# Relation-weighted graph layers on Trainium2: edge sums that run on over tiles

## The chip, the cores and the metric

One Trainium2 chip, of which one core is used. The metric is the device time of one execution in microseconds (us), the median of the runs shown. Less is better. The kernel is written in Bass and Tile: instructions are issued on five engines, PE (TensorE), DVE (VectorE), ACT (ScalarE), POOL (GpSimd) and SP (SyncE, which only issues transfers), and each engine works through its own instructions in order.

## The reference

Four residual blocks on x, 10000 nodes of 512 floats, one after another. Only the first matters here: two graph layers with relations (RGCN) over 5000 edges of two types.

```python
def rgcn_gate_layer(x, row, col, edge_type, basis, att, gate_w, root, bias):
    w = jnp.einsum('rb,bio->rio', att, basis)          # 2 relations, 30 bases of 512 x 512
    x_j = x[col]
    msgs = []
    for r in range(2):
        gate = jax.nn.sigmoid(x_j @ gate_w[r, :, 0])
        msgs.append(gate[:, None] * x_j @ w[r])
    msg = jnp.where((edge_type == 0)[:, None], msgs[0], msgs[1])
    agg = jax.ops.segment_sum(msg, row, num_segments=x.shape[0])
    return agg + x @ root + bias

h   = relu(rgcn_gate_layer(layernorm(x), ..., basis1, att1, gate_w1, root1, bias1))
x   = x + rgcn_gate_layer(h, ..., basis2, att2, gate_w2, root2, bias2)
x   = x + experts(layernorm(x))       # mixture of 16 experts
x   = x + gine(layernorm(x))          # four graph layers over the same edges by target
x   = x + ternary_ffn(layernorm(x))
```

`row` (the target of a sum) is drawn at random and unsorted, so with 10000 nodes and 5000 edges most targets have one edge, or none.

## The kernel before, in words

**The stages.** The profile's windows follow the program: 0 to 534 us a pass over the nodes, with the sorting of the edges and the relation weights between it; 534 to 842 us the edges of layer 1; 842 to 1096 us the edges of layer 2; after that the second node pass, the experts, four GINE layers and the ternary network, which the diff doesn't touch.

**The node pass.** `rgcn_nodes1` (L725) goes over 20 blocks `b` of 512 nodes. Each loads `x_in`, stores it unchanged to `a2_d` (L733; layer 2's sums are added to these rows later), normalizes it, stores the result to `xn_d`, transposes it, multiplies it by `root` (L742), adds the bias on POOL (L748) and stores to `r1_d`, to which layer 1's sums are added later.

**The relation weights.** `relation_weights` (L625) loads the 30 bases of a layer, 1 MB each, and adds each, times a coefficient, to the weights of both relations on DVE (L635 and L637, 128x2048 elements an instruction, two for a basis).

**Sorting.** `sort_edges` puts the edges in a table by relation and target (`by_src`), and again by target alone for the GINE layers (`by_dst`). The table's 128-row tiles are whole tiles of one relation: the second relation starts on a new tile, so there are `RT = ET + 1 = 41` tiles. `add_targets` makes `sidx`, the row that each edge slot adds to: the first slot of a target within a tile takes the target's row, every other slot a spare row behind the nodes, `N` + partition. `place_nodes` is a generator, taken in small steps between other work; it orders the nodes for the GINE layers.

**The edges.** `rgcn_edges` (L640) runs the same loop for both layers. A tile's way, in the functions' names:

- `fetch(t)`: POOL gathers 128 source rows of 512 floats into `x` (L614).
- `make_ready(t)`: in layer 2 a relu on ACT (L665); two products with the gates on DVE that also sum (`prod`, L669); sigmoid on ACT (L674, `g`); the gate of the edge's own relation on DVE (L675, `dots`); PE transposes the keys (L680, `ps_k`); DVE compares and scales (L682): `same[i, j]` is edge i's gate where edges i and j of the tile have one target, and zero elsewhere.
- `add_up(t)`: PE multiplies `x` by `same` (L689), which sums the edges of a target within the tile and leaves the sums transposed; ACT copies them to `aT` (L693).
- `put(t)`: PE multiplies `aT` by the weights of the tile's relation (L703; a register holds which), ACT copies the product to `o` (L708), POOL adds its rows to DRAM with an indirect DMA (`scatter_add`, L619): to `r1_d` in layer 1, to `a2_d` in layer 2.

A target whose edges lie in two tiles is added to by two scatters. All scatters of a layer write one DRAM tensor, so each waits until the one before it has landed.

The loop's iteration `i` issues `fetch(i)`, `add_up(i - 5)`, `put(i - 6)`, `make_ready(i - 3)`, then perhaps a step of `place_nodes`. For PE, POOL, ACT and DVE the order within this loop is kept as written (`manual_schedule`). SP's order, and everything outside these loops, is the scheduler's: it places the sorting and the weights among the node pass. Some 30 of the 116 adding operations at L637 stood among layer 1's first tiles, the others before.

Of the kernel before, what the change touches and what calls it, by code (L numbers as in the profile page):

```python
# [17 lines left out]
P = 128  # L18
N = 10000
D = 512  # L20
# [5 lines left out]
EDGE_SLOTS = ET * P  # L26
LO = 256
HI = (N + LO - 1) // LO
RT = ET + 1

PAIRS = [(p * 1024, 512) for p in range(N // 1024)] + [(N // 1024 * 1024, N % 1024 // 2)]
PT = 8
# [10 lines left out]
CAP = 625  # L43
CT = (CAP + P - 1) // P
LAYERS = 4
FETCHED, READY = 6, 3
LN_EPS = 1e-5
BN_EPS = 1e-5
# [21 lines left out]
def gnn_ffn_kernel(ctx: ExitStack, tc: tile.TileContext, I, out, dram):  # L70
# [7 lines left out]


    xn_d = dram("xn_d", [N, D])  # L80
    r1_d = dram("r1_d", [N + P, D])
    a2_d = dram("a2_d", [N + P, D])
    xf_d = dram("xf_d", [N + P, D])
    x2_d = dram("x2_d", [N + P, D])
    xg_d = dram("xg_d", [N, D])
# [41 lines left out]
    nc.vector.memset(eps_t, LN_EPS)  # L127

    def clear_spare(zero, d):
        nc.sync.dma_start(d[N:, :], zero)  # L130


    def rows_to(sb, d, b, store=False):
# [83 lines left out]
    def sort_edges(tag, key_d, partner_d, attr_d, table, wk, ps, keep, by_relation=False):  # L217
# [77 lines left out]
        if by_relation:  # L295

            first_r = wk.tile([P, P], F32, name="first_r")
            nc.vector.tensor_scalar(off[:, 1:2], ip, float(HI), None, op0=OP.is_lt)
            nc.vector.tensor_scalar(first_r, ones, off[:, 1:2], None, op0=OP.mult)
            ps_o = ps.tile([P, LO], F32, name="ps_s")  # L300
            nc.tensor.matmul(ps_o[:hr, :1], lhsT=first_r[:hr, :hr], rhs=total[:hr], start=True, stop=True)
            n_i = wk.tile([P, 3], I32, name="n_i")
            nc.vector.tensor_scalar(n_i[:hr, 0:1], ps_o[:hr, :1], float(P - 1), None, op0=OP.add)
            nc.vector.tensor_scalar(n_i[:hr, 1:2], n_i[:hr, 0:1], 7, None, op0=OP.logical_shift_right)
            nc.vector.tensor_scalar(n_i[:hr, 2:3], n_i[:hr, 1:2], 7, None, op0=OP.logical_shift_left)
            nc.vector.tensor_copy(off[:hr, 1:2], n_i[:hr, 2:3])
# [62 lines left out]
        nc.vector.tensor_copy(gidx, srt[:, :, 1])  # L369
        return dict(meta, key=key, gidx=gidx, attr=srt[:, :, 2])  # L370

    def add_targets(meta, wk, ps, keep):

        key = meta["key"]
        first = wk.tile([P, RT], F32, name="before")
        equal_keys(key, RT, below, first, wk, ps)
        w = wk.tile([P, RT], F32, name="w_se")
        nc.vector.tensor_scalar(first, first, 0.0, None, op0=OP.is_equal)
        nc.vector.tensor_scalar(w, key, float(N), None, op0=OP.is_lt)
        nc.vector.tensor_mul(first, first, w)  # L380
        spare = wk.tile([P, RT], F32, name="spare")
        nc.vector.tensor_scalar(spare, ip.to_broadcast([P, RT]), float(N), None, op0=OP.add)
        nc.vector.tensor_sub(w, key, spare)
        nc.vector.tensor_mul(w, w, first)
        nc.vector.tensor_add(w, w, spare)
        sidx = keep.tile([P, RT], I32, name="sidx")
        nc.vector.tensor_copy(sidx, w)
        return dict(meta, sidx=sidx)

    def place_nodes(meta, wk, ps, keep):  # L390

# [6 lines left out]

        key = meta["key"]
        tno = irow[:, :ET]  # L400

        ends = wk.tile([P, 2, ET], F32, name="ends")
        for i, sel in enumerate((first_sel, last_sel)):
            ps_l = ps.tile([P, LO], F32, name="ps_s")
            nc.tensor.matmul(ps_l[:, :ET], lhsT=sel, rhs=key, start=True, stop=True)
            nc.vector.tensor_copy(ends[:, i], ps_l[:, :ET])
        carried = keep.tile([P, 4, ET], F32, name="carried")
        co, stays, passes, enters = (carried[:, i] for i in range(4))
        nc.vector.memset(carried, 0.0)
        nc.vector.tensor_tensor(co[:, : ET - 1], ends[:, 1, : ET - 1], ends[:, 0, 1:], OP.is_equal)  # L410
        nc.vector.tensor_scalar(stays, co, -1.0, 1.0, op0=OP.mult, op1=OP.add)

        nc.vector.tensor_tensor(passes, ends[:, 0], ends[:, 1], OP.is_equal)
        nc.vector.tensor_mul(passes, passes, co)
        nc.vector.tensor_mul(passes[:, 1:], passes[:, 1:], co[:, : ET - 1])
        nc.vector.tensor_sub(enters[:, 1:], co[:, : ET - 1], passes[:, 1:])
        yield

        ahead = wk.tile([P, ET], F32, name="ahead")
# [203 lines left out]


    def relation_weights(basis, att_d, pool, stream, tag):  # L625
        att = row_broadcast(pool, att_d, RELATIONS * BASES, f"att_{tag}")
        ws = pool.tile([P, RELATIONS, KC * D], F32, name=f"w_{tag}")
        for b in range(BASES):
            t = stream.tile([P, KC, D], F32, name="basis")
            nc.sync.dma_start(t, basis[b].rearrange("(k p) o -> p k o", p=P))  # L630
            tf = t.rearrange("p k o -> p (k o)")
            for r in range(RELATIONS):
                c = att[:, r * BASES + b : r * BASES + b + 1]
                if b == 0:
                    nc.vector.tensor_scalar(ws[:, r], tf, c, None, op0=OP.mult)  # L635
                else:
                    nc.vector.scalar_tensor_tensor(ws[:, r], tf, c, ws[:, r], op0=OP.mult, op1=OP.add)  # L637
        return ws

    def rgcn_edges(tag, meta, src_d, relu, ws, gate_d, dst_d, beside, take):  # L640

        with ExitStack() as s:
# [11 lines left out]
            got, ready, sums = {}, {}, {}  # L656

            def fetch(t):
                got[t] = wk.tile([P, D], F32, name="x", bufs=FETCHED + 2)
                gather(got[t], src_d, meta["gidx"][:, t : t + 1])  # L660

            def make_ready(t):
                x, kt = got[t], meta["key"][:, t : t + 1]
# [21 lines left out]
            def add_up(t):  # L685
# [6 lines left out]
                sums[t] = wk.tile([P, KC, P], F32, name="aT")  # L692
                nc.scalar.copy(sums[t], ps_a)  # L693

            def put(t):
                aT = sums.pop(t)
                w0 = nc.values_load(
# [8 lines left out]
                    )  # L706
                o = wk.tile([P, D], F32, name="o")
                nc.scalar.copy(o, ps_o)  # L708
                scatter_add(dst_d, meta["sidx"][:, t : t + 1], o)

            E_ = mybir.EngineType
            with tc.manual_schedule(engines={E_.PE, E_.Pool, E_.Activation, E_.DVE}):
                for i in range(RT + FETCHED):
                    if i < RT:
                        fetch(i)
                    if i >= FETCHED - 1 and i - FETCHED + 1 < RT:
                        add_up(i - FETCHED + 1)
                    if i >= FETCHED:
                        put(i - FETCHED)
                    if READY <= i < RT + READY:  # L720
# [31 lines left out]

    with ExitStack() as s:
        wpool = s.enter_context(tc.tile_pool(name="w_rel", bufs=1))
        stream = s.enter_context(tc.tile_pool(name="stream", bufs=2))
        src_meta = s.enter_context(tc.tile_pool(name="src_meta", bufs=1))
        wk = s.enter_context(tc.tile_pool(name="sort", bufs=1))
        place_wk = s.enter_context(tc.tile_pool(name="place_wk", bufs=1))
# [1 line left out]
        with ExitStack() as n:  # L760
# [18 lines left out]
                meta_pool,  # L779
            )  # L780
            rgcn_nodes1(root, bias, (ld, tp, small, pt, po))
            ws = relation_weights(I["L0_gnn_basis1"], I["L0_gnn_att1"], wpool, stream, "1")
        placing = place_nodes(by_dst, place_wk, ps, meta_pool)
        rgcn_edges(
            "1", by_src, xn_d, False, ws, I["L0_gnn_gate_w1"], r1_d, placing,
            lambda i: i >= FETCHED and i % 2 == 0,
        )
        ws = relation_weights(I["L0_gnn_basis2"], I["L0_gnn_att2"], wpool, stream, "2")
        rgcn_edges("2", by_src, r1_d, True, ws, I["L0_gnn_gate_w2"], a2_d, placing, lambda i: True)
        for _ in placing:  # L790
            pass

# [1081 lines left out]
```

## Time and profile before

| what | value |
|---|---|
| median of 3 runs | 4619.68 us (4619.44 to 4631.54) |
| profiled execution | 4620.11 us, span 4618.3 us |
| mean granted TensorE clock | 0.937 of full speed |
| busy: PE, PEld, DVE | 4021.0, 2037.0, 2799.6 us (87%, 44%, 61%) |
| busy: ACT, POOL | 1723.0, 1548.1 us (37%, 34%) |
| weights L637 (DVE) | 116 operations, 316.3 us |
| `put` L703 (PE) | 656 matmuls of both layers, 304.1 us |

The profiled execution is one execution seen by the hardware profiler; its span goes from the first to the last recorded instruction. Matmuls overlap each other and their ends are modelled, so that PE's busy share overstates how full it is. In the rows, `x12` is a count, `128x512<-128x512` are partitions by elements out and in, and what stands in brackets at a row's end is the idle time of the engine before it and what ended that: another engine's instruction, a DMA, or "issue", for which the profile shows no wait. DVE is VectorE, PEld the loading of weights into PE. The granted clock is the share of full speed that TensorE was allowed.

### The profile page before, as it was taken

What the parts mean: (1) busy time and instruction counts of PE and PEld (TensorE: products, weight loads), DVE (VectorE), ACT (ScalarE), POOL (GpSimd) and SP (SyncE); (2) the same over time, 40 slices, a digit from 0 to 9 for tenths busy, and PEclk for the clock granted to TensorE, in tenths of its full rate; (3) what the DMA queues carried; (4) which work ended last, traced back from release to release, by engine and by line L of the source; (5) the groups of instructions that cost most, each with busy time, mean ns of one, the idle gap of its engine ahead of it and who ended that gap; (6) DMA issues with size and microseconds to landing.
All of it is one profiled execution on the core that took longest, in us unless ns stands there. A gap on an engine that the chain in (4) does not pass through costs nothing.

```text
span 4618.3 us, 42924 instructions
## 1 busy us (share of the span) xinstructions
PE 4021.0 (87%) x13624; PEld 2037.0 (44%) x13624; DVE 2799.6 (61%) x5886; ACT 1723.0 (37%) x3086; POOL 1548.1 (34%) x1124
## 2 busy tenths in 40 slices
PE   6799568897999953996879999999999999999997
PEld 3443234443444421443444545545455455544443
DVE  7888865553545455655765546654576455755776
ACT  4334112232333311114544523344233532335775
POOL 3434334342000034785563113311142111422443
PEclk9899789898989875998989999999999999999998
DMA  8777755456555422897621123102231012311332
GB/s 281 232 259 248 226 127 89 83 105 169 197 170 182 158 64 59 160 162 208 199 71 51 73 77 116 47 19 80 83 111 38 28 76 107 89 31 48 110 112 97
DMA packets 294560, 558.83 MB, mean 121 GB/s; under 512 B 41376, under 2 KB 72129, under 8 KB 293311
## 3 DMA queue, kind: packets, MB, share of 16 engines
q1 hardware_dynamic: 221072, 367.30, 23.5%
q0 software_dynamic: 73264, 188.79, 17.7%
q8 instruction: 111, 1.82, 0.2%
q14 instruction: 113, 0.93, 0.1%
HBM read 295.03 MB, written 260.95 MB: 120 GB/s over the span
## 4 chain that ended last, share of the span: by engine, by line
PE 37%; DVE 9%; DMA 3%; issue 2%; ACT 2%; POOL 1%; POOLq 0%; DVEq 0%; ACTq 0%; SPq 0%
PE ps_b L1340 15%; PE ps_d L1340 9%; PE ps_o L1646 5%; PE ps_e L1340 4%; PE ps_x L1482 2%; PE ps_x L1268 2%; DVE stats L1455 2%; DMA x<-xg_d,gpos 1%; DVE feat L1272 1%; DMA x_in<-x_d,node_at 1%; PE ps_q L1714 1%; DVE feat L1355 1%; DVE x L1257 1%; DVE t L1386 1%; POOL e L1261 1%
## 5 line engine op out<-in xcount | busy, mean ns | idle before, releaser
L1340 PE MATMUL ps_b<-feat,w 128*128 128x512 f32 (+1 forms) x1120 | 499.1, 588 | 6.9 <-ACT feat L1468 6.9
L1340 PE MATMUL ps_d<-feat,w_s 128*128 128x512 f32 (+1 forms) x1096 | 490.7, 584 | 2.2 <-DVE feat L1387 1.3
L1348 ACT ACTIVATE feat<-ps_b,cols 128x512 f32<-128x512 f32 (+1 forms) x300 | 204.1, 682 | 535.2 <-PE ps_b L1340 522.5
L1394 POOL TENSOR_TENSOR feat<-feat 128x1024 f32<-128x1024 f32 (+1 forms) x70 | 162.7, 2324 | 627.0 <-DVE feat L1393 601.9
L637 DVE SCALAR_TENSOR_TENSOR w<-basis,att,w 128x2048 f32<-128x2048 f32 x116 | 316.3, 2736 | 14.9 <-DMA basis<-in_L_gnn_basis 14.9
L742 PE MATMUL ps_o<-root,xT 128*128 128x512 f32 (+1 forms) x632 | 322.2, 622 | 0.0
L1409 POOL TENSOR_TENSOR feat<-feat,p 128x1024 f32<-128x1024 f32 (+1 forms) x66 | 166.7, 2525 | 449.2 <-ACT feat L1348 449.0
L1340 PEld LDWEIGHTS ps_b<-feat,w 128*128 128x128 f32 x1120 | 209.9, 192 | 240.8 <-issue 209.5
L703 PE MATMUL ps_o<-w,aT 128*128 x656 | 304.1, 608 | 0.0
L1484 DVE TENSOR_TENSOR x_rows<-ps_x,be 128x512 f32<-128x512 f32 (+1 forms) x237 | 157.5, 685 | 232.3 <-PE ps_x L1482 232.0
L918 PE MATMUL ps_n<-root,rT 128*128 128x512 f32 (+1 forms) x632 | 288.9, 613 | 0.0
L1340 PEld LDWEIGHTS ps_d<-feat,w_s 128*128 128x128 f32 x1096 | 198.4, 191 | 194.2 <-issue 173.0
L1340 PE MATMUL ps_b<-t,w_s 128*128 128x512 f32 (+1 forms) x560 | 253.2, 592 | 26.1 <-ACT feat L1348 26.1
L614 POOL DMA_INDIRECT x<-xg_d,gpos x160 | 175.6, 1098 | 260.8 <-PE ps_x L1268 50.8
L1340 PE MATMUL ps_e<-feat,w 128*128 128x512 f32 (+1 forms) x560 | 253.9, 592 | 9.3 <-DVE feat L1303 9.3
L1340 PE MATMUL ps_b<-feat,w_s 128*128 128x512 f32 (+1 forms) x560 | 250.0, 585 | 0.0
L1468 ACT ACTIVATE feat<-feat,bn_sm 128x512 f32<-128x512 f32 (+2 forms) x320 | 238.0, 808 | 3.6 <-DVE bn_sm L1446 3.6
L1455 DVE BATCH_NORM_STATS2 stats<-feat 128x6 f32<-128x512 f32 (+1 forms) x320 | 203.6, 667 | 41.4 <-POOL feat L1409 28.3
L1268 PEld LDWEIGHTS ps_x<-same,x 128*128 128x128 f32 x1280 | 165.5, 197 | 110.7 <-ACT x L1263 48.8
L1268 PE MATMUL ps_x<-same,x 128*128 128x128 f32 x1280 | 172.9, 284 | 46.8 <-ACT x L1263 33.1
L170 DVE BATCH_NORM_STATS2 ln_st<-x_in 128x6 f32<-128x512 f32 (+1 forms) x237 | 159.6, 683 | 63.0 <-DMA x_in<-x_d,node_at 59.0
L1263 ACT ACTIVATE x<-x 128x512 f32<-128x512 f32 x160 | 98.9, 628 | 242.4 <-DVE x L1257 174.2
(492 smaller groups left out, 7649.4 us busy)
## 6 DMA issues: line engine op xcount, KB each, us to landing
basis<-in_L_gnn_basis SPq DMA_DIRECT2D x60, 1024.0 KB
xg_d<-x_rows SPq DMA_DIRECT2D x234, 256.0 KB
xg_d<-x_in SPq DMA_DIRECT2D x39, 512.0 KB
x_in<-in_x SPq DMA_DIRECT2D x19, 1024.0 KB
a_d<-x_in SPq DMA_DIRECT2D x19, 1024.0 KB
xn_d<-xn SPq DMA_DIRECT2D x19, 1024.0 KB
r_d<-o_nodes SPq DMA_DIRECT2D x19, 1024.0 KB
r_in<-r_d SPq DMA_DIRECT2D x19, 1024.0 KB
```

The lines of the kernel that those rows point to most:

```text
L614: return nc.gpsimd.indirect_dma_start(out=dst, out_offset=None, in_=src, in_offset=bass.IndirectOffsetOnAxis(ap=idx, axis=0))
L637: nc.vector.scalar_tensor_tensor(ws[:, r], tf, c, ws[:, r], op0=OP.mult, op1=OP.add)
L703: nc.tensor.matmul(ps_o, lhsT=aT[:, k, :], rhs=w_all[:, bass.ds(w0 + k * D, D)], start=k == 0, stop=k == KC - 1,)
L742: nc.tensor.matmul(ps_o[:n], lhsT=xT[:, k, a * P : a * P + n], rhs=root[:, k, :], start=k == 0, stop=k == KC - 1,)
L918: nc.tensor.matmul(ps_o[:n_], lhsT=rT[:, k, a * P : a * P + n_], rhs=root[:, k, :], start=k == 0, stop=k == KC - 1,)
L1268: nc.tensor.matmul(ps_a[:, k, :], lhsT=x[:, k * P : (k + 1) * P], rhs=same, start=True, stop=True)
L1340: nc.tensor.matmul(ps[fo], lhsT=A[a][:, k, fo * P : (fo + 1) * P], rhs=x[:, k, :], start=first and k == 0, stop=k == 1, skip_group_check=True,
L1348: nc.scalar.activation(dst[:, fo, :], ps[fo], func, bias=b, scale=scale)
L1409: (nc.vector if last else nc.gpsimd).tensor_tensor(b22, b22, p5, OP.add)
L1455: nc.vector.bn_stats(stats[:, k, 2 * p + j, :], big[:, k, s0 + j * w : s0 + (j + 1) * w])
L1468: nc.scalar.activation(hb, hb, AF.Relu, bias=sm[:, fo, 3:4], scale=sm[:, fo, 2:3])
L1646: nc.tensor.matmul(ps_o[:n_], lhsT=big[:, kc, t * P : t * P + n_], rhs=W2[kc], start=kc == 0, stop=kc == KC - 1,)
```

## The change

It has four parts.

1. **Sums run on over tiles.** Between the two relations there is now one wholly empty tile (`RT` is 42). `add_targets` finds by the first and last key of each tile whether a target goes on into the next tile (`ends_of` and `carries`, taken out of `place_nodes`). A new step `carry(t)` in `rgcn_edges` adds the running sum of the last tile to the first column of `aT`, or hands it on, with two DVE instructions of 128x4. Slots whose target goes on into the next tile take a spare row, so that each target is added to by one scatter alone. Spare rows are two sets of 128, for odd and even tiles. Each scatter is declared independent of the one before it.
2. **Plain rows copied DRAM to DRAM.** `rgcn_nodes1` no longer stores `x_in` to `a2_d`. In layer 1's loop, 40 transfers of 250 rows (512 KB) on SP's queue copy x to `a2_d`; the i-th waits for gather i.
3. **Bases.** `relation_weights` returns a generator. All 30 bases of layer 1 and `EARLY_BASES = 24` of layer 2 are issued ahead of the edges, the last six in iterations 8, 14, 20, ... of layer 1's loop. There are three buffers for bases instead of two. The steps of `place_nodes` go to the odd iterations of layer 1 and to each of layer 2.
4. **POOL's order** in the edge loops is left to the scheduler; PE, ACT and DVE keep the written one.

```diff
-RT = ET + 1
+RT = ET + 2
+EARLY_BASES = 24
-    r1_d = dram("r1_d", [N + P, D])
-    a2_d = dram("a2_d", [N + P, D])
+    r1_d = dram("r1_d", [N + 2 * P, D])
+    a2_d = dram("a2_d", [N + 2 * P, D])
...
-            nc.vector.tensor_scalar(n_i[:hr, 0:1], ps_o[:hr, :1], float(P - 1), None, op0=OP.add)
+            nc.vector.tensor_scalar(n_i[:hr, 0:1], ps_o[:hr, :1], float(2 * P - 1), None, op0=OP.add)
...
+    def ends_of(key, tiles, wk, ps):
+        ends = wk.tile([P, 2, tiles], F32, name="ends")
+        for i, sel in enumerate((first_sel, last_sel)):
+            ps_l = ps.tile([P, LO], F32, name="ps_s")
+            nc.tensor.matmul(ps_l[:, :tiles], lhsT=sel, rhs=key, start=True, stop=True)
+            nc.vector.tensor_copy(ends[:, i], ps_l[:, :tiles])
+        return ends
+
+    def carries(ends, tiles, keep, tag):
+        carried = keep.tile([P, 4, tiles], F32, name=f"carried_{tag}")
+        co, stays, passes, enters = (carried[:, i] for i in range(4))
+        nc.vector.memset(carried, 0.0)
+        nc.vector.tensor_tensor(co[:, : tiles - 1], ends[:, 1, : tiles - 1], ends[:, 0, 1:], OP.is_equal)
+        nc.vector.tensor_scalar(stays, co, -1.0, 1.0, op0=OP.mult, op1=OP.add)
+        nc.vector.tensor_tensor(passes, ends[:, 0], ends[:, 1], OP.is_equal)
+        nc.vector.tensor_mul(passes, passes, co)
+        nc.vector.tensor_mul(passes[:, 1:], passes[:, 1:], co[:, : tiles - 1])
+        nc.vector.tensor_sub(enters[:, 1:], co[:, : tiles - 1], passes[:, 1:])
+        return carried

     def add_targets(meta, wk, ps, keep):
         key = meta["key"]
+        both = wk.tile([P, RT], F32, name="key_rel")
+        nc.vector.tensor_scalar(both, meta["attr"], 0.0, 2.0 * SENT, op0=OP.not_equal, op1=OP.mult)
+        nc.vector.tensor_add(both, both, key)
+        ends = ends_of(both, RT, wk, ps)
+        carried = carries(ends, RT, keep, "s")
         first = wk.tile([P, RT], F32, name="before")
         equal_keys(key, RT, below, first, wk, ps)
         w = wk.tile([P, RT], F32, name="w_se")
+        nc.vector.tensor_tensor(w, both, ends[:, 1], OP.is_equal)
+        nc.vector.tensor_mul(w, w, carried[:, 0])
+        nc.vector.tensor_add(first, first, w)
...
+        odd = wk.tile([P, RT], I32, name="odd")
         spare = wk.tile([P, RT], F32, name="spare")
-        nc.vector.tensor_scalar(spare, ip.to_broadcast([P, RT]), float(N), None, op0=OP.add)
+        nc.vector.tensor_scalar(odd, row_i[:, :RT], 1, None, op0=OP.bitwise_and)
+        nc.vector.tensor_copy(spare, odd)
+        nc.vector.tensor_scalar(spare, spare, float(P), ip, op0=OP.mult, op1=OP.add)
+        nc.vector.tensor_scalar(spare, spare, float(N), None, op0=OP.add)
...
     def relation_weights(basis, att_d, pool, stream, tag):
...
-        for b in range(BASES):
...
-        return ws
+        def sums():
+            for b in range(BASES):
...
+                yield
+        return ws, sums()

-    def rgcn_edges(tag, meta, src_d, relu, ws, gate_d, dst_d, beside, take):
+    def rgcn_edges(tag, meta, src_d, relu, ws, gate_d, dst_d, beside):
...
+            acc = fix.tile([P, KC], F32, name="acc_0")
+            nc.vector.memset(acc, 0.0)
+            carry_on = {-1: acc}
...
+            def carry(t):
+                aT, last = sums[t], carry_on.pop(t - 1)
+                carry_on[t] = wk.tile([P, KC], F32, name="acc")
+                for dst, src, i in ((carry_on[t], P - 1, 2), (aT[:, :, 0], 0, 3)):
+                    nc.vector.scalar_tensor_tensor(
+                        dst, last, meta["carried"][:, i, t : t + 1], aT[:, :, src], op0=OP.mult, op1=OP.add
+                    )
...
-                scatter_add(dst_d, meta["sidx"][:, t : t + 1], o)
+                st = scatter_add(dst_d, meta["sidx"][:, t : t + 1], o)
+                if stores:
+                    tc.declare_no_dep(st.ins, stores[-1].ins, reason="they have different rows")
+                stores.append(st)

-            with tc.manual_schedule(engines={E_.PE, E_.Pool, E_.Activation, E_.DVE}):
+            with tc.manual_schedule(engines={E_.PE, E_.Activation, E_.DVE}):
                 for i in range(RT + FETCHED):
                     if i < RT:
-                        fetch(i)
+                        fetched = fetch(i)
                     if i >= FETCHED - 1 and i - FETCHED + 1 < RT:
                         add_up(i - FETCHED + 1)
                     if i >= FETCHED:
                         put(i - FETCHED)
                     if READY <= i < RT + READY:
                         make_ready(i - READY)
-                    if take(i):
-                        next(beside, None)
+                    if i >= FETCHED - 1 and i - FETCHED + 1 < RT:
+                        carry(i - FETCHED + 1)
+                    beside(i, fetched)

     def rgcn_nodes1(root, bias, pools):
...
-            rows_to(x, a2_d, b, store=True)
...
-        stream = s.enter_context(tc.tile_pool(name="stream", bufs=2))
+        stream = s.enter_context(tc.tile_pool(name="stream", bufs=3))
...
-            ws = relation_weights(I["L0_gnn_basis1"], I["L0_gnn_att1"], wpool, stream, "1")
+            ws1, adding = relation_weights(I["L0_gnn_basis1"], I["L0_gnn_att1"], wpool, stream, "1")
+            for _ in adding:
+                pass
+            ws2, adding = relation_weights(I["L0_gnn_basis2"], I["L0_gnn_att2"], wpool, stream, "2")
+            for _ in range(EARLY_BASES):
+                next(adding)
         placing = place_nodes(by_dst, place_wk, ps, meta_pool)
+        def beside_1(i, ready):
+            if i > FETCHED and i % 6 == 2:
+                next(adding, None)
+            elif i > FETCHED and i % 2:
+                next(placing, None)
+            if i < ET:
+                c0, c1 = N * i // ET, N * (i + 1) // ET
+                cp = nc.sync.dma_start(a2_d[c0:c1, :], I["x"][c0:c1, :])
+                tc.add_manual_dep(
+                    cp.ins, ready.ins.name,
+                    mybir.DependencyInfo(mybir.DependencyClass.Sync, mybir.DependencyReason.DATA),
+                    reason="not all at once, and not beside the nodes",
+                )
+        rgcn_edges("1", by_src, xn_d, False, ws1, I["L0_gnn_gate_w1"], r1_d, beside_1)
+        for _ in adding:
+            pass
         rgcn_edges(
-            "1", by_src, xn_d, False, ws, I["L0_gnn_gate_w1"], r1_d, placing,
-            lambda i: i >= FETCHED and i % 2 == 0,
+            "2", by_src, r1_d, True, ws2, I["L0_gnn_gate_w2"], a2_d, lambda i, _: next(placing, None)
         )
-        ws = relation_weights(I["L0_gnn_basis2"], I["L0_gnn_att2"], wpool, stream, "2")
-        rgcn_edges("2", by_src, r1_d, True, ws, I["L0_gnn_gate_w2"], a2_d, placing, lambda i: True)
```

In the built order of the changed kernel, 104 of the adding operations stand before the first edge tile, against 86 before; POOL has ten gathers ahead and then takes gathers and scatters in turn.

More of the change, by code (lines that the diff above doesn't have):

```diff
@@ L129, in clear_spare @@
     def clear_spare(zero, d):
-        nc.sync.dma_start(d[N:, :], zero)
+        for r0 in range(N, d.shape[0], P):
+            nc.sync.dma_start(d[r0 : r0 + P, :], zero)
     def rows_to(sb, d, b, store=False):
@@ L387, in add_targets @@
         nc.vector.tensor_copy(sidx, w)
-        return dict(meta, sidx=sidx)
+        return dict(meta, sidx=sidx, carried=carried)
     def place_nodes(meta, wk, ps, keep):
@@ L400, in place_nodes @@
         tno = irow[:, :ET]
[L402 to L416, printed above, removed]
+        ends = ends_of(key, ET, wk, ps)
+        carried = carries(ends, ET, keep, "d")
+        co = carried[:, 0]
         yield
@@ L627, in relation_weights @@
         ws = pool.tile([P, RELATIONS, KC * D], F32, name=f"w_{tag}")
-        for b in range(BASES):
[L629 to L637, printed above, removed]
-        return ws
-    def rgcn_edges(tag, meta, src_d, relu, ws, gate_d, dst_d, beside, take):
+        def sums():
+            for b in range(BASES):
+                t = stream.tile([P, KC, D], F32, name="basis")
+                nc.sync.dma_start(t, basis[b].rearrange("(k p) o -> p k o", p=P))
+                tf = t.rearrange("p k o -> p (k o)")
+                for r in range(RELATIONS):
+                    c = att[:, r * BASES + b : r * BASES + b + 1]
+                    if b == 0:
+                        nc.vector.tensor_scalar(ws[:, r], tf, c, None, op0=OP.mult)
+                    else:
+                        nc.vector.scalar_tensor_tensor(ws[:, r], tf, c, ws[:, r], op0=OP.mult, op1=OP.add)
+                yield
+        return ws, sums()
+    def rgcn_edges(tag, meta, src_d, relu, ws, gate_d, dst_d, beside):
         with ExitStack() as s:
@@ L654, in rgcn_edges @@
             w_all = ws.rearrange("p r w -> p (r w)")
-            got, ready, sums = {}, {}, {}
+            got, ready, sums, stores = {}, {}, {}, []
+            acc = fix.tile([P, KC], F32, name="acc_0")
+            nc.vector.memset(acc, 0.0)
+            carry_on = {-1: acc}
             def fetch(t):
                 got[t] = wk.tile([P, D], F32, name="x", bufs=FETCHED + 2)
-                gather(got[t], src_d, meta["gidx"][:, t : t + 1])
+                return gather(got[t], src_d, meta["gidx"][:, t : t + 1])
             def make_ready(t):
```

## The prediction

> **What bounds the kernel now.** I read the windows by stage first, since the change stays inside the first 1096 us.
>
> ```profile
> 0.00:534.00 534.00, 439.02 (x1480) 205.77 (x1480) 434.75 (x862) 197.13 (x420) 204.04 (x112) 0.94 0.75 250
> 534.00:842.00 308.00, 214.15 (x780) 116.85 (x780) 188.14 (x494) 53.81 (x124) 120.65 (x83) 0.87 0.54 121
> 842.00:1096.00 254.00, 216.41 (x836) 115.83 (x836) 130.52 (x482) 73.95 (x164) 107.90 (x82) 0.92 0.50 93
> ```
>
> The rows are the node pass, layer 1's edges and layer 2's edges; behind the length come busy PE, PEld, DVE, ACT and POOL, the granted clock, the DMA share and GB/s. No engine fills an edge stage, so I read POOL in order of time there.
>
> ```profile
> 831.17 1.55 POOL L619 DMA_INDIRECT r_d<-o,sidx  x1 [3.97 <-issue]
> 836.66 1.55 POOL L619 DMA_INDIRECT r_d<-o,sidx  x1 [3.95 <-DMA r_d<-o,sidx]
> ```
>
> Each scatter starts when the one before has landed: 5.5 us apart, 5.7 with a gather between. Layer 2's 41 run from 861.86 to 1091.19, 5.73 us each, while PE finished its last product at 1074. So the scatters' chain sets the edge stages. One tile of layer 2 in order of time shows what stands behind it:
>
> ```profile
> 917.14 0.27 PE L680 MATMUL ps_k<-ident,key_s 128*128 128x128 f32 x1
> ...
> 917.39 0.59 ACT L708 COPY o<-ps_o 128x512 f32<-128x512 f32 x1 [1.77 <-issue]
> ...
> 917.87 0.64 ACT L665 ACTIVATE x<-x 128x512 f32<-128x512 f32 x1
> ...
> 918.54 0.69 DVE L669 SCALAR_TENSOR_TENSOR prod<-x,gate 128x512 f32<-128x512 f32 x1 [1.32 <-ACT x L665]
> ...
> 918.83 3.60 PE L703 MATMUL ps_o<-w,aT 128*128 x8
> ...
> 920.07 0.20 ACT L674 ACTIVATE g<-dots 128x2 f32<-128x2 f32 x1 [1.56 <-DVE prod L669]
> ...
> 920.30 0.16 DVE L675 SCALAR_TENSOR_TENSOR dots<-g,of_rel 128x2 f32<-128x2 f32 x1 [0.33 <-ACT g L674]
> ...
> 920.58 0.41 DVE L682 TENSOR_SCALAR same<-ps_k,key_s,g 128x128 f32<-128x128 f32 x1
> 920.91 0.47 DVE L567 TENSOR_SCALAR_CACHE_REDUCE waste_p<-ps_r,wanted 128x256 bf16<-128x256 f32 x1
> ...
> 922.27 0.27 PE L680 MATMUL ps_k<-ident,key_s 128*128 128x128 f32 x1
> 922.51 0.59 ACT L708 COPY o<-ps_o 128x512 f32<-128x512 f32 x1 [1.77 <-issue]
> ```
>
> PE repeats after 5.13 us with no wait: `put` begins 918.83, while `same` comes only at 920.58. It may: `same` is for two tiles on.
>
> **The change, part by part.**
>
> *Scatters.* In the built order a scatter now waits for the one two before it: a floor of 5.5 / 2 = 2.8 us a tile. POOL needs 1.58 + 1.0 + 0.6 = 3.2. Both drop off the path.
>
> *Carry, the new wait.* Two small DVE operations stand behind `same` of tile t+2 and before `put` of tile t. `put` waits for the second. `same` waits for the sigmoid on ACT, which in ACT's order stands behind the copy of tile t-1's product. So `put` t-1, copy, sigmoid, `same`, carry, `put` t is a ring with no slack. From the rows: product start to copy 3.68 (918.83 to 922.51); copy to relu 0.48; relu to first prod 0.67; to sigmoid 1.53; to dots 0.23; to same 0.28; to the next DVE operation 0.33; two carries 0.33 (a 128x4 operation of this kind takes 0.216, L1276, overlapped); to PE 0.20. Layer 2's period is 7.73 us. In layer 1 there is no relu and the prods run ahead, so copy to sigmoid is 0.48 and the period 5.53.
>
> Behind the waiting `put` nothing else on PE can run; it idles 7.73 - 5.13 = 2.6 us per tile. What that does to the clock:
>
> ```profile
> 765.33 0.62 PE L488 MATMUL ps_s<-incl_p,less_next 40*41 40x256 f32 x2 [2.29 <-DVE less_next L486]
> ...
> 765.93 1.88 PE L689 MATMUL ps_a<-same,x 128*128 128x128 f32 x8
> 767.60 4.58 PE L703 MATMUL ps_o<-w,aT 128*128 x8
> 772.02 0.27 PE L680 MATMUL ps_k<-ident,key_s 128*128 128x128 f32 x1
> 772.13 1.06 PE L689 MATMUL ps_a<-same,x 128*128 128x128 f32 x8
> 773.03 3.60 PE L703 MATMUL ps_o<-w,aT 128*128 x8
> ```
>
> After 2.29 us idle the same matmuls lose 0.82 + 0.98 = 1.8 us; gaps of 1.5 to 1.75 us here (798.35, 787.35, 753.73) lose next to nothing; of the gaps between 2.2 and 3.1 us in the trace some two thirds were followed by such a loss. The loss lies partly in `put`, on the ring. I take half of it, 0.9 us; ends 0 and 1.8.
>
> [...] The rows above show a loss at 2.29 us, so I keep it.
>
> *Layer 2's sum.* First gather to first copied product 18.8 (842.22 to 861.00) + 0.6; 39 periods of 7.73 + 0.9 = 337; two last ones, with nothing left to make ready, 5 each; 0.7 to the last scatter: 367 against 249 (842.22 to 1091.19): +118. Ends: 332 (+83) without clock loss, 402 (+153) with all of it. The placing steps fit into DVE's 4.8 us between carry and prod.
>
> *Layer 1.* The last 30 of 116 adding operations stood among its first tiles (8.4 us a tile and more until 621). Now three tiles are made ready in 2.7 each, then table load 1.3, carry 0.6 and a cold product 4.6: first prod to first copy 14.6 against 23.1 (538.04 to 561.13): -8.5. Then 41 intervals: 14 plain of 5.5; 6 with a basis, where two sums of 2.34 push the prods 1.7 late: 7.25; 10 with four key comparisons, which PE needs before its next products: 7.15 (6.95 now, 636.80 to 643.75); eleven others together 77, built likewise from 725 to 826 plus the ring. Sum 269, and 11 for the clock beside the bases and comparisons: 280. So the last scatter starts 538 + 14.6 + 280 + 0.7 = 833 against 836.66: -3; ends -20 and +30. The extra tile is in the counts.
>
> *Rows copied beside.* 40 copies of 512 KB. In layer 1's window the hardware queue took 15.2% for 15.63 MB, 3.0 us per MB: 61 us for 20.5 MB. With the gathers' and scatters' 38.6% (119 us) and six bases that is about 200 of 295 us of DMA time: hidden, as gathers run nine tiles ahead. At double that price the share is 0.9, and scatters have 11 us each to land: still hidden, else the +30. On SP, layer 2's last three bases stand behind copies 26, 32 and 38; each is used some iterations later.
>
> *Node pass.* 20.5 MB of stores go, and SP's waits on x_in before them (109 us in all, none of them PE's). Eighteen more sums of 2.34 come onto DVE: +42 on its 435 busy us of 534. That and a start of 25 us and one wait of 12 for the sorted table give a floor of 514 for the first prod, 538 now. PE waits there for DVE, not for DMA. I take -8; ends -24 and +20.
>
> Added sorting operations on 128x42 (0.2 us each, about fifteen) go under the ends. From 1096 us on the order is the same.
>
> **Sum.** -8 - 3 + 118 = +107 us. The profiled execution took 4620.11 (span 4618.3), 0.4 over the median of 4619.68: 4727.
>
> **Rivals.**
> - *A: the ring without clock loss.* [...] Layer 2 +83, layer 1 -14, node pass -8: +61, 4681.
> - *B, faster: `put` does not wait.* If carry is done before PE has made the next tile's sums, that is, within 1.7 us of a product's end, the path is PE's own work: 36 x 5.13 + 5 x 4.5 = 207 in layer 2 (-22), 5.6 x 41 = 230 in layer 1 (-54), node pass -8: -84, 4536. Against: relu and prods alone put `same` 3.3 us after the product's end.
> - *C: the copies choke layer 1,* scatters landing after over 11 us: at 8 us a tile +50 more, 4777. Against: 0.54 DMA share now.
> - *The scatters still chained* (the change not doing what it says): then nothing is gained, but the ring is longer than 5.7 anyway: as forecast.
>
> **Numbers.** Forecast 0.6, A 0.25, B 0.07, C 0.06, else 0.02. The range takes the ends of the clock and the node pass: 4650 to 4790. A measurement of this kernel tells 0.3% (14 us) from no change: faster 0.08, same 0.03, slower 0.89.
>
> **What would show it.** Right: layer 2's scatters 7.7 to 9.5 us apart, PE's products waiting for the carry on DVE, the clock in that window below 0.92, layer 1 ending within 20 us of now. Wrong: layer 2's products 5.1 us apart, or PE waiting for a DMA.

## The result, and the profile after

| | before | changed |
|---|---|---|
| median of 4 runs | 4625.61 us | 4770.31 us (4759.76 to 4778.72) |
| ratio | 1 | 1.0311, interval 1.0281 to 1.0341 |
| profiled execution, span | 4618.3 us | 4772.0 us |
| mean granted clock | 0.937 | 0.932 |

The changed kernel is 3.1% slower, by 145 us where 107 were forecast; the time lies in the range. The profiled executions differ by 153.7 us. Cut at the first gate product, the last scatter of layer 1, the first gather and the last scatter of layer 2, the difference lies here:

| stage | before | changed | difference | forecast |
|---|---|---|---|---|
| to the first gate product | 538.04 | 556.54 | +18.5 | -8 |
| to layer 1's last scatter | 298.6 | 299.3 | +0.7 | -3 |
| to layer 2's first gather | 5.6 | 5.6 | 0 | 0 |
| to layer 2's last scatter | 249.0 | 368.4 | +119.4 | +118 |
| to the end | 3527.1 | 3542.2 | +15.1 | 0 |

The last stage has the same work in the same order, but for one thing: preparing the ternary network's weights (8 us of small operations) now starts behind layer 2's last scatter and not ahead of it. That shifts little, since the second node pass's first product comes 15.9 us after that scatter where it came after 15.0. In the profiles of the nine kernels below the stage took between 3508.5 and 3542.9 us, so its 15 us are no more than what executions differ by; what makes them differ is not shown.

The windows of the changed kernel, columns as in the prediction's first fence:

```profile
0.00:553.00 553.00, 451.00 (x1485) 211.01 (x1485) 472.29 (x901) 197.39 (x420) 203.11 (x113) 0.93 0.69 229
553.00:861.00 308.00, 231.68 (x791) 126.96 (x792) 158.78 (x562) 55.83 (x127) 117.56 (x85) 0.90 0.62 153
861.00:1234.00 373.00, 261.64 (x850) 132.18 (x849) 140.60 (x561) 75.86 (x168) 108.22 (x84) 0.88 0.34 60
```

In layer 2 (third row) the clock fell from 0.92 to 0.88 and the DMA share from 0.50 to 0.34; between the first and the last product (876 to 1229 us) no wait is put down to a transfer. One tile of it in order of time, the lines that answer to the tile shown of before:

```profile
1002.97 0.59 ACT L750 COPY o<-ps_o 128x512 f32<-128x512 f32 x1 [4.47 <-issue]
1003.46 0.64 ACT L699 ACTIVATE x<-x 128x512 f32<-128x512 f32 x1
...
1004.12 0.69 DVE L703 SCALAR_TENSOR_TENSOR prod<-x,gate 128x512 f32<-128x512 f32 x1 [3.73 <-ACT x L699]
...
1005.65 0.20 ACT L708 ACTIVATE g<-dots 128x2 f32<-128x2 f32 x1 [1.56 <-DVE prod L703]
...
1006.16 0.41 DVE L716 TENSOR_SCALAR same<-ps_k,key_s,g 128x128 f32<-128x128 f32 x1
1006.49 0.21 DVE L733 SCALAR_TENSOR_TENSOR acc<-acc,carried_s,aT 128x4 f32<-128x4 f32 x1
1006.62 0.22 DVE L733 SCALAR_TENSOR_TENSOR aT<-acc,carried_s,aT 128x4 f32<-128x4 f32 x1
...
1006.99 5.37 PE L745 MATMUL ps_o<-w,aT 128*128 x8 [2.41 <-DVE aT L733]
...
1012.44 0.59 ACT L750 COPY o<-ps_o 128x512 f32<-128x512 f32 x1 [6.11 <-issue]
```

Read it downwards: the product's copy releases the relu, this the gate products, these the sigmoid, then `same`, then the two carries (L733), and the second releases the next product, after PE has stood for 2.41 us. At 1012.44 the round begins again. From one scatter to the next it is about 7.77 us in 17 of layer 2's 39 full periods and 9.46 in 22: in the longer ones the product took 5.37 us, as here, instead of 3.67. In the last eight full periods, which have no placing step, PE has less to do and stands 3.09 us instead of 2.41; the period stays the same, as it must if the ring sets it. The view of the products' line in this window says who held them:

```profile
its engine sat idle before it (us, times) until:
  ACT aT L727: 106.3, 39
  DVE aT L733: 100.4, 40
```

The second line is the matmuls', held by the carry. The first is that of the loads of `aT` into PE (PEld), which the view puts down to an ACT copy of sums. That copy cannot be what ends the wait: in the tile shown it was done at 1006.33 and is the next tile's, this tile's sums had been copied at 997.94, and the load starts at 1006.96, 0.12 us after the carry's end, beside the product.

### The profile page after: what moved, and what is told of

Read it like the earlier page. It is cut to its first block, busy times and chain, and to the rows that moved or that the text cites. A ratio compares the mean times of both kernels' runs of the same rounds, so it can differ in the third digit from the quotient of the medians.

```text
span 4772.0 us, 43364 instructions
## 1 busy us (share of the span) xinstructions
PE 4108.1 (86%) x13663; PEld 2073.6 (43%) x13663; DVE 2817.0 (59%) x6089; ACT 1726.5 (36%) x3093; POOL 1544.2 (32%) x1128
## 4 chain that ended last, share of the span: by engine, by line
PE 36%; DVE 8%; DMA 3%; ACT 2%; issue 2%; POOL 1%; POOLq 0%; DVEq 0%; ACTq 0%
PE ps_b L1405 14%; PE ps_d L1405 8%; PE ps_o L1711 5%; PE ps_e L1405 4%; PE ps_x L1547 2%; PE ps_x L1333 2%; DMA x<-xg_d,gpos 2%; DVE stats L1520 1%; DMA x_in<-x_d,node_at 1%; ACT feat L1533 1%; DVE feat L1337 1%; PE ps_q L1779 1%; DVE x L1322 1%; DVE feat L1420 1%; ACT feat L1413 0%
## 5 line engine op out<-in xcount | busy, mean ns | idle before, releaser
L745 PE MATMUL ps_o<-w,aT 128*128 x672 | 359.3, 685 | 125.3 <-DVE aT L733 123.0
L665 DVE SCALAR_TENSOR_TENSOR w<-basis,att,w 128x2048 f32<-128x2048 f32 x116 | 303.1, 2624 | 0.0
L745 PEld LDWEIGHTS ps_o<-w,aT 128*128 128x128 f32 x672 | 140.8, 220 | 290.1 <-issue 156.9
L703 DVE SCALAR_TENSOR_TENSOR prod<-x,gate 128x512 f32<-128x512 f32 x168 | 115.9, 690 | 208.7 <-ACT x L699 196.4
```

What stands on the lines that cost most here:

```text
L745: nc.tensor.matmul(ps_o, lhsT=aT[:, k, :], rhs=w_all[:, bass.ds(w0 + k * D, D)], start=k == 0, stop=k == KC - 1,)
```

## The experiments

Stage lengths are from each kernel's profile, ratios against the kernel before on the same chip. Four runs with the changed kernel's order of the node pass (it, `warm`, `warm9`, `chained`) had their first gate product between 554.7 and 556.5 us, `carry_first` and `copy_behind` at 559.3 and 562.5: differences of a few us in that stage say nothing.

| kernel | ratio (interval) | first product | layer 1 | layer 2 |
|---|---|---|---|---|
| changed | 1.0311 (1.0281 to 1.0341) | 556.5 | 299.3 | 368.4 |
| carry_first | 0.9938 (0.9913 to 0.9962) | 559.3 | 272.7 | 221.5 |
| copy_behind | 0.9938 (0.9919 to 0.9957) | 562.5 | 265.9 | 224.7 |
| chained | 1.0042 (1.0027 to 1.0058) | 554.7 | 293.0 | 252.1 |
| warm | 1.0309 (1.0283 to 1.0335) | 555.9 | 298.9 | 371.8 |
| warm9 | 1.0228 (1.0212 to 1.0244) | 555.8 | 302.2 | 336.8 |
| early13 | 1.0327 (1.0302 to 1.0352) | 528.1 | 330.6 | 368.4 |
| stores_back | 1.0324 (1.0309 to 1.0340) | 560.2 | 303.5 | 368.6 |
| before_three | 0.9995 (0.9983 to 1.0007) | 560.0 | 282.8 | 242.2 |
| open_ring | 0.9847 (0.9833 to 0.9860) | 531.5 | 239.2 | 233.3 |

### The ring, opened on DVE

```diff
+                    if i >= FETCHED - 1 and i - FETCHED + 1 < RT:
+                        carry(i - FETCHED + 1)
                     if READY <= i < RT + READY:
                         make_ready(i - READY)
-                    if i >= FETCHED - 1 and i - FETCHED + 1 < RT:
-                        carry(i - FETCHED + 1)
                     beside(i, fetched)
```

> The changed kernel, with carry(t) written ahead of make_ready(t+2) on DVE instead of behind it; nothing else differs. Theory (a ring of product, copy, relu, sigmoid, same, carry, next product): the carry then waits only for the copied sums, which PE finishes before the product of the tile before, so layer 2's scatters come 5.1 to 5.3 us apart instead of 7.77 and 9.46 (first gather to last scatter 368 -> about 232 us), layer 1's plain tiles 5.1 instead of 5.57; the whole about 4590 us. Rival 1 (the scatters, still landing one behind the other, set the pace): no tile under 5.5. Rival 2 (DVE has too much to do): no shorter than now.

Two lines changed places, and layer 2 went from 368.4 to 221.5 us, 27.5 less than in the kernel before too: scatters 5.12 us apart, 4.44 where no placing step is left. Layer 1's plain tiles went from 5.57 to 4.44. The expected 4590 us or so was made against 4770; on this run's chip the kernel took 4576.8, the kernel before 4605.06. A tile of layer 2:

```profile
932.74 0.21 DVE L733 SCALAR_TENSOR_TENSOR aT<-acc,carried_s,aT 128x4 f32<-128x4 f32 x1
...
932.89 0.59 ACT L750 COPY o<-ps_o 128x512 f32<-128x512 f32 x1 [1.77 <-issue]
...
934.34 3.60 PE L745 MATMUL ps_o<-w,aT 128*128 x8
...
936.08 0.41 DVE L716 TENSOR_SCALAR same<-ps_k,key_s,g 128x128 f32<-128x128 f32 x1
```

The carry for the product of 934.34 is issued at 932.74, before the copy of the product ahead of it; PE's row has no bracket, so it did not wait. Both rivals fall.

### The same ring, opened on ACT

```diff
 put(t):      the copy o <- ps_o and the scatter taken out, into put_out(t)
                     if READY <= i < RT + READY:
                         make_ready(i - READY)
+                    if i >= FETCHED:
+                        put_out(i - FETCHED)
                     if i >= FETCHED - 1 and i - FETCHED + 1 < RT:
                         carry(i - FETCHED + 1)
```

> The changed kernel, with the ACT copy of the product and the scatter written behind make_ready instead of ahead of it; DVE's order is that of the changed kernel (carry behind same). Theory: the ring goes through ACT's order, since relu and sigmoid stand behind the copy of the tile before. With the copy behind them it is open at another place, and only the transposed keys, which PE makes behind the product, still tie same to it: 3.7 + 0.3 + 0.2 + 0.3 + 0.3 + 0.3 + 0.2 = 5.3 us a tile in layer 2, the whole some 130 to 150 us shorter than the changed kernel. Rival (the two carry operations cost DVE too much): 7.7 to 9.5 as now.

DVE's order is that of the changed kernel; layer 2 took 224.7 us at 5.12 a tile:

```profile
931.10 0.41 DVE L716 TENSOR_SCALAR same<-ps_k,key_s,g 128x128 f32<-128x128 f32 x1 [0.41 <-PE ps_k L714]
...
931.56 0.22 DVE L733 SCALAR_TENSOR_TENSOR aT<-acc,carried_s,aT 128x4 f32<-128x4 f32 x1
...
932.47 3.60 PE L745 MATMUL ps_o<-w,aT 128*128 x8
```

The carry still stands behind `same`, which now waits for PE's keys, but it is done before PE comes to the product. So it is not the two small DVE operations that cost 120 us, nor their place alone, but that ACT's written order tied `same` to the copy. The 5.3 of the expectation was for the way through the keys; PE's own 5.12 is all that shows. The gain over the changed kernel, 0.9938 for 1.0311 or some 170 us, is more than the 130 to 150 expected: layer 1, 33 us shorter, had not been counted.

### What the scatters' wait was worth

`chained` is `carry_first` without `declare_no_dep`.

> carry_first with the scatters no longer declared independent, so that each waits again until the one before has landed. Theory (that wait was a floor of its own, 5.5 to 5.7 us a tile): layer 2 is 5.55 us a tile instead of 5.12, 18 to 25 us longer than carry_first's 221.5; layer 1's plain tiles 5.5 instead of 4.44, with less than that in the sum, since its long tiles cover it. If the scatters' independence is worth nothing behind the open ring, it stays at 5.12.

Layer 2 took 252.1 us, 5.65 us in the median tile, and layer 1 293.0: 30.6 and 20.3 us more than `carry_first`. That is what the first part of the change takes away, once nothing longer stands behind it. With the ring closed, freeing the scatters can show no gain: 7.77 covers 5.6.

### The clock's share

```diff
                 ps_o = po.tile([P, D], F32, name="ps_o")
+                if relu:
+                    for _ in range(16):        # warm; 9 in warm9
+                        nc.tensor.matmul(ps_o[:, :P], lhsT=ident, rhs=ident, start=True, stop=True)
                 for k in range(KC):
```

> The changed kernel with 16 matmuls of 128x128 written to the product's own PSUM tile ahead of each product of layer 2 and overwritten by it: they do nothing but fill some 2.0 of the 2.4 us in which PE waits for the carry. Theory (part of the 7.77 and 9.46 us is the granted clock that falls after the gaps): every tile takes 7.77, layer 2 loses about 40 us, its clock is over 0.95. Rival (the longer tiles are longer for another wait): 7.77 and 9.46 stay mixed as they are, or every tile gets longer.

> warm with 9 filling matmuls instead of 16. In warm each of the 16 took 0.22 us and not the 0.13 reckoned with, 3.6 us together, so that they were a longer path than the wait that they filled (8.70 us a tile at a clock of 0.98). Nine take 2.0 us of the 2.41 us gap. Theory (the 9.46 us tiles are 1.69 us longer for the clock after the gap): every tile 7.77, layer 2 some 30 to 42 us shorter than 368, clock above 0.95. Rival: 9.46 and 7.77 stay mixed.

`warm` missed: the 16 took 3.57 us (8.70 against 5.13 a tile), and PE's own work became the path. It only shows periods of 8.7 throughout, without the mixture, at a clock of 0.98. `warm9` settles it:

```profile
1002.28 2.17 PE L746 MATMUL ps_o<-ident 128*128 128x128 f32 x18
1004.85 3.67 PE L748 MATMUL ps_o<-w,aT 128*128 x8 [0.40 <-DVE aT L733]
```

PE still waits for the carry, but 0.40 us (an estimate of 1.1 for the tiles without a placing step, which stand 3.09 - 2.41 = 0.68 us longer in the changed kernel), and all but three of the full periods are 7.72 to 7.78. Layer 2 is 31.6 us shorter with matmuls that compute nothing, the clock 0.97. The difference of the longer tiles, 22 x 1.69 = 37 us, was the clock; the fillers gave some back, since layer 2's two last tiles grew from 4.33 and 3.43 to 6.34 and 5.44 and its first scatter came 1.7 us later.

Which products are slow, the granted clock in the changed kernel's profile shows. Between 877 and 1226 us it changes 45 times between full and half, and each change lies a whole number of stretches of 3.41 us behind the first, to within 0.01 us. It stood at half for 22 single stretches, one on each of the 22 slow products. Four stretches in a row (columns as in the windows above):

```profile
987.05:990.46 3.41, 1.00 (x5) 0.54 (x4) 2.90 (x14) 0.68 (x2) 2.08 (x2) 1.00 0.54 59
990.46:993.88 3.42, 3.42 (x5) 1.35 (x4) 0.41 (x3) 0.00 (x0) 0.00 (x0) 0.50 0.34 94
993.88:997.29 3.41, 2.88 (x16) 1.57 (x14) 0.95 (x3) 1.12 (x2) 1.09 (x1) 1.00 0.01 2
997.29:1000.70 3.41, 1.48 (x4) 0.79 (x5) 2.63 (x12) 0.68 (x2) 1.48 (x2) 1.00 0.74 105
```

The gap from 987.29 to 989.70 lies in one stretch: PE is busy for 1.00 us of it, and the next stretch is granted half. The gap from 996.76 to 999.22 is cut at 997.29: PE is busy for 2.88 and 1.48 us of the two stretches, and the product behind it runs at full clock. So it is between 877 and 1226 us throughout: PE was busy for at most 0.39 of each stretch ahead of one at half, and for at least 0.42 of each of the 57 full ones with another full one behind. These are counts of one profile; no run shows that they hold elsewhere.

### The node pass

`early13` has `EARLY_BASES = 13` and a basis in every even iteration of layer 1.

> The changed kernel with EARLY_BASES = 13, so that 86 adding operations stand ahead of the edges as in the kernel before, and a basis in each even iteration of layer 1. Theory (the node pass is as long as DVE's work in it): the first gate product of layer 1 comes at 536 to 542 us instead of 556.5, layer 1 gets about 11 x 1.7 = 19 us longer, the whole stays within 10 us. Rival (the node pass grew because of the order of SP's transfers or the sorting): the first product stays at 550 to 560.

The first product came at 528.1, earlier than expected, and layer 1 took 31 us longer, more than the 19 expected. What a basis does to a tile of layer 1 is the same in both kernels; in the changed one:

```profile
710.46 4.61 DVE L665 SCALAR_TENSOR_TENSOR w<-basis,att,w 128x2048 f32<-128x2048 f32 x2
...
718.02 0.94 PE L213 MATMUL ps_s<-ident,key_d 128*128 128x128 f32 x2 [3.33 <-DVE eq L214]
...
720.46 5.47 PE L745 MATMUL ps_o<-w,aT 128*128 x8
```

The sums push the gate products, `same` and the key comparisons behind them, PE waits 3.33 us for the first comparison (1.76 without sums), and the product after that runs slow. Such a tile takes 11.6 us, against 7.2 or, where the clock falls there too, 8.9 with comparisons alone. Over the whole, the two stages cancel. `early13` has 82 of the adding operations ahead of the edges, four fewer than the kernel before, and not as many as the expectation says. Where the node pass's 28 us went, POOL and SP show. First the changed kernel, then `early13`:

```profile
530.95 2.43 POOL L792 TENSOR_TENSOR o_nodes<-o_nodes,bias 16x512 f32<-16x512 f32 x1 [0.83 <-ACT o_nodes L790]
...
542.35 0.37 SPq L658 DMA_DIRECT2D basis<-in_L_gnn_basis  x1
...
542.77 0.74 SPq L141 DMA_DIRECT2D r_d<-o_nodes  x1
...
552.95 1.02 POOL L639 DMA_INDIRECT x<-xn_d,gidx_s  x1 [19.57 <-DMA r_d<-o_nodes]
```

```profile
519.67 2.70 SPq L141 DMA_DIRECT2D r_d<-o_nodes  x2
...
520.77 1.25 POOL L792 TENSOR_TENSOR o_nodes<-o_nodes,bias 16x512 f32<-16x512 f32 x1 [1.13 <-ACT o_nodes L790]
...
524.65 1.02 POOL L639 DMA_INDIRECT x<-xn_d,gidx_s  x1 [2.63 <-issue]
```

The last bias addition, the end of PE's work, comes 10 us earlier. And from there to the first gather it is 2.6 us instead of 19.6: in the changed kernel the last stores to `r1_d` stand on SP's queue behind loads of bases, and those wait for a buffer, that is, for DVE's sums (25.6 us in four waits of SP between 500 and 556 us). In `early13` the last sum ahead of the edges starts at 448.4, so no load is left in the way. The kernel before, whose sums run on to the edges, waited 20.3 us there too. The changed kernel's 18.5 us are PE's end, which came 19.1 us later (530.95 against 511.86), with the same wait behind it.

`stores_back` undoes the second part of the change.

> The changed kernel without the DRAM to DRAM copies: the node pass stores x_in to a2_d again, as the kernel before did. Theory of the prediction (the node pass is DVE's, stores and copies are hidden): first gate product within 8 us of the changed kernel's 556.5, layer 1 from there to its last scatter within 5 us of 299, layer 2 unchanged at 368. What early13 showed (528 with the same sums as before, where the kernel before had 538) speaks for another: the stores cost the node pass about 10 us, so that the first product comes at about 566. Rival (copies beside the edges hold up gathers or scatters): layer 1 gets over 10 us shorter.

Layer 1 took 303.5 us: the copies hold up nothing beside the edges, though they raise its DMA load (81 GB/s without, 153 with). The node pass took 560.2 us, 3.6 more, which is within what profiles of the same order differ by. This does not price the stores cleanly, as the scheduler also placed the sums and the sorting elsewhere: there the last bias addition comes at 509.5, 21 us earlier than in the changed kernel and with the same 104 sums, but DVE's sums run on to 560.2, right up to the first gate product.

> The kernel before, with three buffers for bases instead of two; nothing else differs. early13, with as many sums ahead of the edges as the kernel before, had its first gate product at 528 us, the kernel before at 538; stores_back shows that the stores of x_in are not what makes the difference (560 and 556.5, where the six profiles with the changed kernel's own node pass run from 554.7 to 562.5). Theory: the third buffer does, since DVE waited 9.1 us for bases in the node pass of the kernel before and not at all in the changed one: the first product comes at 527 to 531, and the whole is some 8 us shorter. Rival (the order in which the scheduler places the sums and the sorting): it stays at 535 or more.

This theory fell. DVE did not wait for bases any more, but the first product came at 560.0, 22 us later than before, with 94 sums ahead of it instead of 86, to the very end. Layer 1 then was 15.8 us and layer 2 6.8 us shorter, the whole the same. Where the sums end early, PE's end sets the first product (last sum started at 448 us: 528; at 475 in `open_ring`: 531). Where they run on, the product comes with their end (the kernel before 538, `before_three` and `stores_back` 560) or, in the changed kernel, 10 us behind it, with DVE idle until the first gather, which waits for the stuck stores. So it goes with the scheduler's order, not with buffers or stores alone. What each of these does by itself stays open, and so does why PE's end moves between 509 and 536.

### A version that beats both

The conditions ahead of the calls are left out.

```diff
                     add_up(i - FETCHED + 1)
+                    beside(i, fetched)
                     put(i - FETCHED)
-                    make_ready(i - READY)
-                    carry(i - FETCHED + 1)
-                    beside(i, fetched)
+                    carry(i - FETCHED + 1)
+                    make_ready(i - READY)
...
-                yield
+                    yield          # one adding operation a step, not two
...
-EARLY_BASES = 24
+EARLY_BASES = 16
...
-            for _ in range(EARLY_BASES):
+            for _ in range(RELATIONS * EARLY_BASES):
...
-            if i > FETCHED and i % 6 == 2:
-                next(adding, None)
-            elif i > FETCHED and i % 2:
-                next(placing, None)
+            if FETCHED < i < 31 and i % 2:
+                next(placing, None)
+            elif i > FETCHED:
+                next(adding, None)
```

> carry_first, and the step taken beside (node placing or a basis) written between add_up and put, where PE has just left DVE nothing to wait for; one adding operation an iteration instead of two in every sixth, 16 bases of layer 2 ahead of the edges instead of 24, node placing in twelve odd iterations of layer 1. Theory: the first gate product comes some 16 x 1.5 = 25 us earlier than carry_first's 559; layer 1's iterations with a sum take 4.6 instead of 6.95 and those with four key comparisons 5.5 instead of 7 to 11, so that layer 1 takes 205 to 230 us instead of 273; layer 2 about 215 to 222. Together some 4500 to 4540 us where the kernel before has 4605. Rival (DVE, with a sum in every second iteration and more, falls behind its period and holds back the carry): layer 1 stays at 260 or more.

The median of 4557.35 us is 1.5% under the kernel before and 4.5% under the changed one (0.9847 / 1.0311 = 0.955); the expected 4500 to 4540 stood against 4605, which is 0.977 to 0.986, so it came in at the upper end, with the first product 28 us earlier than `carry_first`'s, but layers 1 and 2 some 10 us longer than expected. Layer 1 took 239.2 us: as long as sums and placing steps alternate, iterations with one sum take 4.44, as `carry_first`'s plain ones, so there the sums are hidden wholly; those with key comparisons take 6.93 and not 5.5, since PE still waits once for DVE:

```profile
621.75 0.38 PE L213 MATMUL ps_s<-ident,key_d 128*128 128x128 f32 x2
623.17 0.32 PE L213 MATMUL ps_s<-ident,key_d 128*128 128x128 f32 x1 [1.04 <-DVE eq L214]
```

One placing step, a chain between PE and DVE, cost a tile of 17.8 us, and layer 2 began later than `carry_first`'s (25.7 us from its first gather to its first scatter, 19.3 there).

## Why the prediction was right, and where it was off

The ring and its period were right, and with them the largest term. The profiles differ by 46.7 us more than forecast: 26.5 in the node pass, 15.1 in the rest, 3.7 in layer 1 and 1.4 in layer 2.

- *The scatters leave the path*: shown. With the ring open, tiles go at 4.44 to 5.12 us, below the old chain's 5.6, and at the layers' ends scatters follow at 3.43.
- *The ring*: shown, twice, at its DVE and at its ACT link. The 7.73 us of the rows were 7.77, layer 1's 5.53 were 5.57. The layer's 367 us were 368.4.
- *The clock, half of 1.8 us*: the mean period was 8.73, so 0.96 for the forecast 0.9. That this fits is in part luck: half was taken because some of the loss was thought to lie off the ring; measured was all of it on the ring, 1.69 us, in the 22 of 39 periods that had a stretch at half clock and none in the others, though PE's gap was 2.4 to 3.1 us in both. `warm9` shows the price, 31.6 us. Rival A falls with it.
- *Layer 1*: +0.7 for -3: first product to first scatter 13.3 us (15.3 reckoned), from there to the last 286.0 (280). Key comparisons alone were as reckoned, 7.21 for 7.15, and 8.9 where the clock fell. The basis, reckoned as 7.25 in a tile of its own, fell together with comparisons and made 11.6 of one tile.
- *The node pass, -8*: the term that failed. It took DVE's busy time as the length of the stage and went near the floor of 514. PE's end came 19.1 us later; that the added sums delayed it is not shown, since `stores_back`, with as many, has it at 509.5. DVE itself stood idle for 9.4 us ahead of the first product. And the wait behind that end, 20 us for stores stuck on SP's queue, was in the trace of before and not in the sum; with the sums out of the way it is 2.6.
- *Rival B* (put does not wait) did not come about, but its price stands: its 227 us for layer 2 (249 - 22) are `carry_first`'s 221.5. Its condition, a carry done before the next tile's sums, is what two exchanged lines give. Its layer 1, 245, missed the comparisons; 272.7 were measured.
- *Rival C* falls: no tile waits for the copies; layer 1 took 299.3 us with them and 303.5 without (`stores_back`).
- *The rest unchanged*: +15.1 us in this profile; the forecast had no room for what executions of the same instructions differ by.

## What to carry to other kernels

When an order is written by hand, put an operation that another engine waits for ahead of those that it does not need: the two carries needed only sums that had long been there, and stood behind a sigmoid that needed the last product. Follow each new wait through all engines' orders until it closes or ends; if it comes back to the instruction that waits, the sum along it is the period, whatever else is made shorter. And when work is moved ahead of a stage's end, look at what else stands on the queue that feeds it.

## What the runs showed of the hardware

- In layer 2 of the changed kernel TensorE stood idle for 2.4 to 3.1 us ahead of the product in each period of 7.8 to 9.5 us, and its granted clock was 0.88 over the layer; a product's eight recorded matmuls took 5.31 to 5.37 us in 22 of the 39 full periods and 3.67 us in 17. In `warm9`, where the gap was 0.40 us in the tile shown, the clock was 0.97 and no full period was longer than 8.05 us.
- In that profile of the changed kernel, between 877 and 1226 us, the clock's 45 changes lay whole stretches of 3.41 us apart. The 22 stretches at half each stood behind one in which TensorE was busy for 0.39 or less; the 57 full ones with another full one behind were busy for 0.42 or more. A gap of 2.41 us within one stretch was followed by half clock, one of 2.46 us cut into 0.53 and 1.93 was not.
- A filling matmul of 128x128 in fp32 took 0.22 us in `warm` (3.57 us for 16, two recorded matmuls each), not the 0.13 read off the rows of `add_up`, where eight recorded matmuls of 1.06 us are four instructions.
